# A four-layer graph-attention kernel: one group's shifted scores and exponentials moved from VectorE to ScalarE, and its log-sum-exp products spread over twice as many steps

## The chip, the cores and the metric

The kernel runs on one core of a Trainium2 chip. The metric is the device time of one execution in microseconds, as the median of several runs. The engines are called as in the profile: PE (TensorE, matrix products), DVE (VectorE), ACT (ScalarE), POOL (GpSimd) and SP (SyncE, which here only starts DMAs). Each engine works through its own list of instructions in order and waits on semaphores that the others raise.

## The reference, cut to what matters

There are B = 8 batches of N = 2048 nodes with F = 64 features, and one 2048 x 2048 adjacency matrix for all of them. Three graph-attention layers follow one another, then a fourth layer with a softmax per feature, and each ends in a residual sum and a layer norm. The change concerns the third attention layer (layer 2 in the code, which counts from 0):

```python
h = jnp.matmul(x, W)
f1 = jnp.einsum('bnf,f->bn', h, a1)
f2 = jnp.einsum('bnf,f->bn', h, a2)
e = jax.nn.leaky_relu(f1[:, :, None] + f2[:, None, :], negative_slope=ALPHA)
e = jnp.where(adj[None, :, :] > 0, e, NEG_BIG)
attention = jax.nn.softmax(e, axis=2)
h_prime = jnp.matmul(attention, h)
```

Its scores can be large, so the kernel needs a bound for each row before it takes exponentials. It gets one from a scaled log-sum-exp: with the largest score of a batch taken off f2 (that gives s2), it takes exp(s2 * scale + 75) for every source node, multiplies these by the 0/1 adjacency matrix on PE, and turns the sums back into a bound for each target node.

## The kernel before

**Tiles and units.** The 2048 nodes are K = 16 blocks of 128, so that a tile holds 128 nodes in its partitions. The adjacency matrix stands in SBUF as `edge`, 128 x 16 x 2048 in fp8. A unit is one layer of one batch, and it has 16 steps, one for each block jb of 128 source nodes. The order of units (`todo`) is layer 0 and layer 1 of batches 0 to 3, layer 0 and layer 1 of batches 4 to 7, and layer 2 of batches 0 to 7. "(0,6)" is layer 0 of batch 6.

**A step.** `reach` calls `weights` (lines 997 to 1005): one DVE instruction of 128 x 2048 makes the weights w of block jb as max(r, low) * edge. r is a row of scores that `spread` (line 843) has laid over all partitions in PSUM, with four small products on PE at the end of the unit before. In layer 2 ACT then takes the exponential of w. `products` (line 1044) multiplies w by the features on PE and sums into two PSUM banks, acc. At step 15 it adds the rows of empty nodes (acc<-emptyT,mean). There are four buffers for w, so DVE can be a few steps ahead of PE.

**Work beside the steps.** Everything else is written as generators, held in `bg`, a list of streams. After each step `bg.step()` (line 1513) lets each stream run to its next `yield`; `yield n` means that it is taken up again n steps later. The instructions go into the engines' lists in just this order and are kept in it (`InOrder`, line 70). So a `yield` decides between which weights instructions of DVE, and between which products of PE, a piece of side work stands. Streams are `features0` (layer 0's features), `finish` (the end of a unit: p_o, o, eh, hb, the layer norm's sq_x and st_x), `scores` (the next layer's scores: p_xT, p_s, se, p_r, then the row), `mask_out` (copies of `edge` to DRAM as float, mf) and `group`. Two PSUM buffers, handed out in order by `pm_slots`, serve all of these. `Banks.width` (line 129) says how many of them `finish` and `transposed` take at once: two, but one while `Banks.busy` is set.

**The group.** Layer 2's batches form two groups of NB = 4: batches 0 to 3 (gi = 0) and 4 to 7 (gi = 1). `group` (line 856) begins when the last `scores` of its batches are done. For the first group that is during layer 0 of batches 4 to 7, and for the second during layer 2. It does, one after the other:

- the largest and smallest f2 of each batch: lc, a transpose p_lc, lt, a product p_lim, and lim in every partition;
- eight small DVE operations on sc, among them the scale sc[:, 1] of each batch;
- s2 = f2 - lim, tt = s2 * sc[:, 1] on DVE, 128 x 64 each, and te = exp(tt + 75) on ACT, which goes into the constant tile `te` in bf16;
- six more DVE operations: down, lo, tt, lo, lo and sc[:, 3];
- a wait until unit 12, which is (1,4), and then the 256 products p_lse<-te,edge, in eight blocks of 32, with a `yield` after each;
- am: six DVE operations that turn the sums into bounds, a transpose p_am, a copy amT on ACT, five POOL operations that split it into three bf16 pieces, and a DMA to rows_d, from which `prepare` loads the row of each batch's layer 2.

While p_lse is held, one of the two PSUM buffers is taken and `Banks.busy` is set.

Of the kernel before, what the change touches and what calls it, by code (L numbers as in the profile page):

```python
# [8 lines left out]
F32 = mybir.dt.float32  # L9
# [5 lines left out]
AF = mybir.ActivationFunctionType  # L15
ALU = mybir.AluOpType
AX = mybir.AxisListType

P = 128
# [31 lines left out]
def gnn4_kernel(ctx: ExitStack, tc: tile.TileContext, t, out):  # L51
# [3 lines left out]
    K = N // P  # L55
# [3 lines left out]
    NB = 4  # L59
# [4 lines left out]
    small = ctx.enter_context(tc.tile_pool(name="small", bufs=2))  # L64
# [76 lines left out]
    pe, dve, act, pool = (InOrder(e) for e in (nc.tensor, nc.vector, nc.scalar, nc.gpsimd))  # L141

    def psum(name):
        return pm.tile([P, 512], F32, tag="pm", name=name)

    def bc_f(v, n=K, f=F):
        return v[:, :, None].to_broadcast([P, n, f])
# [75 lines left out]
    p = psum("p_nodes")  # L223
# [27 lines left out]
    te = consts.tile([P, K, NB], BF16, name="te")  # L251
# [105 lines left out]
    lse_up = consts.tile([P, 1], F32, name="lse_up")  # L357
# [498 lines left out]
    def group(gi):  # L856

        bs = list(range(gi * NB, (gi + 1) * NB))
        g = groups2[gi]
        nm = f"g{gi}"  # L860
        s = g.s
# [6 lines left out]
        p = psum(f"p_lc_{nm}")  # L868
# [7 lines left out]
        p = psum(f"p_lim_{nm}")  # L876
# [7 lines left out]
        yield 1  # L884
        lim = small.tile([P, 2, NB], F32, tag="lim", name=f"lim_{nm}")
        dve.tensor_copy(lim, p[:, : 2 * NB].rearrange("p (a b) -> p a b", a=2))
        pm_slots.give()

        sc = small.tile([P, 4, NB], F32, tag="sc", name=f"sc_{nm}")
# [11 lines left out]
        )  # L901
        yield 1
        g.s2 = small.tile([P, NB, K], F32, tag="s2", name=f"s2_{nm}")
        dve.tensor_tensor(g.s2, s[:, 1], bc_f(lim[:, 0], NB, K), ALU.subtract)
        tt = small.tile([P, NB, K], F32, tag="tt", name=f"tt_{nm}", bufs=1)
        dve.tensor_tensor(tt, g.s2, bc_f(sc[:, 1], NB, K), ALU.mult)
        act.activation(
            te.rearrange("p k b -> p b k"), tt, AF.Exp, bias=lse_up
        )

        g.down = small.tile([P, NB, K], F32, tag="down", name=f"down_{nm}")
        dve.tensor_scalar(g.down, g.s2, -SHIFT, None, ALU.add)
# [16 lines left out]
        p = psum(f"p_lse_{nm}")  # L929
        for ib in range(K):  # L930
            for jb in range(K):
                pe.matmul(
                    p[:, NB * ib : NB * (ib + 1)],
                    lhsT=edge[:, jb, ib * P : (ib + 1) * P],
                    rhs=te[:, jb, :],
                    start=(jb == 0),
                    stop=(jb == K - 1),
                )
            if ib % 2:
                yield 1 if gi else 2  # L940
        dve.tensor_scalar(
            am.rearrange("p b k -> p k b"),
            p[:, : NB * K].bitcast(I32).rearrange("p (k b) -> p k b", b=NB),
# [16 lines left out]
        p = psum(f"p_am_{nm}")  # L960
# [504 lines left out]
    for n, (layer, b) in enumerate(todo):  # L1465
# [10 lines left out]
        for jb in range(K):  # L1476
# [15 lines left out]
            if jb == K - 1:  # L1492
                end = [lambda u=u: finish(u)]
                if layer < 2:
                    end += [2 if now[0] < 2 else 1, lambda layer=layer, b=b: scores(layer + 1, b)]
                else:
                    end += [1, lambda b=b: l3_features(b)]
                if layer == 1 and b % NB == NB - 1:
                    end += [lambda b=b: group(b // NB)]
                bg.add(chain(*end), begun=True, slow=done)  # L1500
            elif not done and jb >= 10 and ready(*nxt):
                prepare(*nxt)
                prepared.add(n + 1)
                done = True
# [524 lines left out]
```

## Time and profile before

| what | value |
|---|---|
| runs | 1358.67 us median of 3 (1357.25 to 1359.91) |
| profiled execution, its own time | 1361.64 us |
| its span, first to last instruction | 1359.8 us |
| mean granted clock of PE | 0.959 |
| busy: PE, DVE, POOL, ACT | 1214.8, 1176.2, 813.9, 752.0 us |
| weights of layers 0 and 1 on DVE | 270 instructions, 550.9 us |
| products of layers 0 and 1 on PE | 2048 records, 495.7 us |
| first group's p_lse blocks | 567.1 to 607.9 us |
| first group's s_g and tt_g on DVE | 501.0 to 505.1 us |

In the profile a tile's name comes without its number, so `acc<-w,pv` is the product of every unit of layers 0 and 1. `s_g` is the group's s2. A line of the timeline gives the start, the duration, the engine, the operation, what it writes and reads, and in brackets the time that the engine stood idle before it and who ended that. All lines of the kernel carry one line number, L80, because every operation goes through one recording helper; one goes by the tiles' names.

### The profile page before, as it was taken

To read this page: it belongs to the slowest core of one execution; us is meant where nothing else is said; L and a number is where in the kernel's file an instruction comes from. 1 tells how busy PE (TensorE), PEld (TensorE's weight loads), DVE (VectorE), ACT (ScalarE), POOL (GpSimd) and SP (SyncE) were. 2 spreads that over 40 slices of the span, in tenths; PEclk is the share of its full clock that TensorE was granted. 3 is DMA by queue.
4 is the path that set the end of the run, shared out by engine and by line. 5 is a ranking of instruction groups with operands and counts; after the bars stand their busy time and mean duration, and the time that the engine had idled before them with its cause. 6 is when DMAs were issued, how large, how long until landed. Compare 5 with 4: busy or idle time off the path is not lost.

```text
span 1359.8 us, 19529 instructions
## 1 busy us (share of the span) xinstructions
PE 1214.8 (89%) x7169; PEld 622.8 (46%) x7169; DVE 1176.2 (87%) x1064; ACT 752.0 (55%) x1370; POOL 813.9 (60%) x1163
## 2 busy tenths in 40 slices
PE   3689897999999979999998889789998899989995
PEld 3333232344343423343333334245654555668895
DVE  3889888999999998789999889898979798978865
ACT  4444443546345553344426978777566767675432
POOL 1665876677879787657763533434464665656443
PEclk9689999999999999799999988899999999999998
DMA  8640000000000222123101000025543545534663
GB/s 292 234 106 1 1 2 1 2 2 2 2 1 1 94 64 81 59 79 96 33 1 39 1 16 1 22 63 147 142 134 94 139 117 140 139 113 140 179 167 80
DMA packets 120651, 102.98 MB, mean 76 GB/s; under 512 B 58877, under 2 KB 91805, under 8 KB 119522
## 3 DMA queue, kind: packets, MB, share of 16 engines
q1 hardware_dynamic: 120178, 101.52, 25.9%
q8 instruction: 59, 0.97, 0.3%
q14 instruction: 46, 0.38, 0.1%
q10 hardware_dynamic: 368, 0.12, 0.0%
HBM read 76.13 MB, written 25.45 MB: 75 GB/s over the span
## 4 chain that ended last, share of the span: by engine, by line
PE 49%; DVE 15%; ACT 7%; issue 7%; POOL 3%; DMA 1%; SPq 0%; DVEq 0%; POOLq 0%; ACTq 0%
PE acc L80 27%; PE p_l L80 14%; DVE w L80 8%; ACT w L80 2%; PE p_o L80 2%; PE p_s L80 2%; DVE o L80 2%; PE r L80 1%; ACT sp L80 1%; DVE x L80 1%; PE p_lse_g L80 1%; DVE nd L80 1%; DVE fs L80 1%; ACT L80 1%; PE p_h L80 1%
## 5 line engine op out<-in xcount | busy, mean ns | idle before, releaser
L80 DVE SCALAR_TENSOR_TENSOR w<-r,se,edge 128x2048 f32<-128x2048 f32 (+1 forms) x270 | 550.9, 2103 | 31.1 <-PE r L80 23.2
L80 PE MATMUL acc<-w,pv 128*64 128x512 f32 x2048 | 495.7, 618 | 41.3 <-DVE w L80 29.6
L80 DVE SCALAR_TENSOR_TENSOR w<-r,lo_g,edge 128x2048 f32<-128x2048 f32 (+1 forms) x144 | 297.3, 2097 | 28.8 <-PE r L80 16.8
L80 ACT ACTIVATE w<-w,down_g 128x2048 f32<-128x2048 f32 (+1 forms) x144 | 257.5, 1810 | 71.5 <-DVE w L80 56.9
L80 PEld LDWEIGHTS p_l<-v,mask 128*128 128x128 f32 x2048 | 252.8, 193 | 60.7 <-issue 46.2
L80 PE MATMUL acc<-w,x 128*64 128x512 f32 x1024 | 258.1, 633 | 25.2 <-ACT w L80 21.8
L80 PE MATMUL p_l<-v,mask 128*128 128x256 f32 x2048 | 268.6, 288 | 10.0 <-ACT mask L80 5.2
L80 PEld LDWEIGHTS acc<-w,pv 128*64 128x64 f32 x2048 | 133.1, 139 | 293.5 <-issue 179.9
L80 POOL TENSOR_TENSOR sq_x<-sq_x 128x32 f32<-128x32 f32 (+4 forms) x207 | 109.8, 531 | 59.1 <-ACT sq_x L80 44.5
L80 PEld LDWEIGHTS acc<-w,x 128*64 128x64 f32 x1024 | 66.2, 142 | 140.6 <-issue 86.1
L80 ACT ACTIVATE o<-p_o,den 128x64 f32<-128x64 f32 x256 | 55.8, 326 | 64.5 <-DVE den L80 64.5
L80 ACT ACTIVATE nd<-p_l,empty 128x256 f32<-128x256 f32 x64 | 29.9, 469 | 81.0 <-PE p_l L80 80.8
L80 PE MATMUL p_o<-rh,oT 128*128 128x130 f32 x384 | 60.5, 294 | 15.5 <-DVE o L80 4.9
L80 ACT COPY oT<-acc 128x512 f32<-128x512 f32 x48 | 25.7, 586 | 85.8 <-PE acc L80 85.8
L80 PEld LDWEIGHTS p_o<-rh,oT 128*128 128x128 f32 x384 | 49.5, 194 | 49.2 <-issue 26.6
L80 POOL TENSOR_TENSOR st_x<-isw_x,mhalf 128x16 f32<-128x16 f32 x24 | 70.3, 2930 | 1.9
L80 POOL TENSOR_SCALAR isw<-isw 128x4 f32<-128x4 f32 x32 | 9.0, 281 | 100.5 <-DVE isw L80 82.1
L80 POOL TENSOR_TENSOR eh<-eh,x 128x1024 f32<-128x1024 f32 (+2 forms) x24 | 36.4, 1530 | 39.5 <-ACT eh L80 35.0
L80 POOL TENSOR_TENSOR d<-x,wa_bc 128x1024 f32<-128x1024 f32 x8 | 19.1, 2382 | 66.5 <-DVE x L80 66.5
L80 DVE RECIPROCAL nd<-nd 128x256 f32<-128x256 f32 x32 | 55.8, 1743 | 0.0
L80 POOL TENSOR_TENSOR sq_x<-o 128x512 f32<-128x512 f32 x23 | 29.2, 1269 | 41.4 <-DVE o L80 41.2
L80 ACT ACTIVATE xs<-x,nodes 128x64 f32<-128x64 f32 x128 | 44.3, 438 | 3.5 <-PE p_xT L80 3.4
(263 smaller groups left out, 1544.4 us busy)
## 6 DMA issues: line engine op xcount, KB each, us to landing
mask<-mask_d SPq DMA_DIRECT2D x192, 256.0 KB
mask_d<-mf SPq DMA_DIRECT2D x32, 512.0 KB
raw<-in_adjT_dram SPq DMA_DIRECT2D x8, 1024.0 KB
raw<-in_adjT_dram SPq DMA_DIRECT2D x16, 512.0 KB
x<-in_x_dram SPq DMA_DIRECT2D x8, 512.0 KB
x_d<-x SPq DMA_DIRECT2D x8, 512.0 KB
e<-x_d SPq DMA_DIRECT2D x64, 64.0 KB
out_dram<-o SPq DMA_DIRECT2D x64, 64.0 KB
```

The costliest lines, as they stand in the source:

```text
L80: ins = f(*args, **kwargs)
```

## The change

For the first group alone, the two DVE operations that make s2 and tt, and the one ACT operation that makes te, are replaced by eight ACT operations of 128 x 16, four for s2 (one per batch, with the negative of the batch's largest score as bias) and four for te (with the batch's scale). The negative comes from one more DVE operation, `away`. A `yield 2` follows, so the six DVE operations after it are issued two steps later. Further down, the pause after each block of log-sum-exp products is four steps in place of two, so the eight blocks stand in units (1,4) and (1,5) and no longer in (1,4) alone; the PSUM buffer is held for as long. The second group stays as it was.

```diff
         yield 1
         lim = small.tile([P, 2, NB], F32, tag="lim", name=f"lim_{nm}")
         dve.tensor_copy(lim, p[:, : 2 * NB].rearrange("p (a b) -> p a b", a=2))
+        if not gi:
+            away = small.tile([P, NB], F32, tag="away", name=f"away_{nm}", bufs=1)
+            dve.tensor_scalar(away, p[:, :NB], -1.0, None, ALU.mult)
         pm_slots.give()
...
         g.s2 = small.tile([P, NB, K], F32, tag="s2", name=f"s2_{nm}")
-        dve.tensor_tensor(g.s2, s[:, 1], bc_f(lim[:, 0], NB, K), ALU.subtract)
         tt = small.tile([P, NB, K], F32, tag="tt", name=f"tt_{nm}", bufs=1)
-        dve.tensor_tensor(tt, g.s2, bc_f(sc[:, 1], NB, K), ALU.mult)
-        act.activation(
-            te.rearrange("p k b -> p b k"), tt, AF.Exp, bias=lse_up
-        )
+        if gi:
+            dve.tensor_tensor(g.s2, s[:, 1], bc_f(lim[:, 0], NB, K), ALU.subtract)
+            dve.tensor_tensor(tt, g.s2, bc_f(sc[:, 1], NB, K), ALU.mult)
+            act.activation(te.rearrange("p k b -> p b k"), tt, AF.Exp, bias=lse_up)
+        else:
+            for b in range(NB):
+                act.activation(g.s2[:, b], s[:, 1, b], AF.Identity, bias=away[:, b : b + 1])
+            for b in range(NB):
+                act.activation(
+                    te[:, :, b], g.s2[:, b], AF.Exp, scale=sc[:, 1, b : b + 1], bias=lse_up
+                )
+            yield 2
...
             if ib % 2:
-                yield 1 if gi else 2
+                yield 1 if gi else 4
```

## The prediction

> **What bounds the kernel now.** I read the page first: its span, the busy shares and the chain that ended last.
>
> ```profile
> span 1359.8 us, 19529 instructions
> ...
> PE 1214.8 (89%) x7169; PEld 622.8 (46%) x7169; DVE 1176.2 (87%) x1064; ACT 752.0 (55%) x1370; POOL 813.9 (60%) x1163
> ...
> PE 49%; DVE 15%; ACT 7%; issue 7%; POOL 3%; DMA 1%; SPq 0%; DVEq 0%; POOLq 0%; ACTq 0%
> ```
>
> PE and DVE are both nearly full, and ACT and POOL are not. In layers 0 and 1 a step of 128 source nodes costs PE 1.87 us (four products, start to start) and DVE 2.26 us (one weights instruction), and PE has further work between steps. So the lead changes hands inside each unit, and an edit must be priced in the unit where it stands. Next I cut the trace into units, a unit being one batch of one layer. The first group's log-sum-exp products lie in (1,4); the next row is (1,5):
>
> ```profile
> 563.52:611.02 47.50, 46.79 (x426) 19.79 (x425) 34.46 (x29) 17.09 (x41) 27.04 (x37) 0.91 0.22 68
> 611.02:651.64 40.62, 38.09 (x193) 14.86 (x192) 37.14 (x25) 17.93 (x48) 26.00 (x42) 1.00 0.26 80
> ```
>
> Columns: stretch, its length, busy us of PE, weight loads, DVE, ACT, POOL, then PE's clock. PE is full in (1,4) and idle 2.5 us in (1,5). The other place is unit (0,6), 482.00 to 522.05, where PE is busy only 32.01 of 40.05 us. There I read the timeline of DVE, of POOL and of PE:
>
> ```profile
> 498.76 2.35 DVE L80 SCALAR_TENSOR_TENSOR w<-r,se,edge 128x2048 f32<-128x2048 f32 x1
> 501.02 2.18 DVE L80 TENSOR_TENSOR s_g<-s,lim_g 128x64 f32<-128x64 f32 x1
> 503.24 1.82 DVE L80 TENSOR_TENSOR tt_g<-s_g,sc_g 128x64 f32<-128x64 f32 x1
> ```
>
> ```profile
> 500.77 2.35 POOL L80 TENSOR_TENSOR o<-o,hb 128x1024 f32<-128x1024 f32 x1
> 503.08 1.90 POOL L80 TENSOR_TENSOR pv<-y,se 128x1024 f32<-128x1024 f32 x1
> 507.55 2.36 POOL L80 TENSOR_TENSOR eh<-eh,x 128x1024 f32<-128x1024 f32 x1 [2.57 <-ACT eh L80]
> 509.88 0.45 POOL L80 TENSOR_SCALAR meanr<-mean,later 128x64 bf16<-128x64 bf16 x1
> 510.42 0.30 POOL L80 TENSOR_TENSOR mean<-mean,meanr 128x64 f32<-128x64 f32 x1
> 510.68 2.35 POOL L80 TENSOR_TENSOR o<-o,eh 128x1024 f32<-128x1024 f32 x1
> ```
>
> ```profile
> 501.16 3.34 PE L80 MATMUL acc<-w,pv 128*64 128x512 f32 x8 [3.70 <-DVE w L80]
> 504.43 0.43 PE L80 MATMUL p_mean<-tree,ones 128*128 128x64 f32 x2
> 508.66 6.41 PE L80 MATMUL acc<-w,pv 128*64 128x512 f32 x16 [3.80 <-DVE w L80]
> ```
>
> The two operations the change takes from DVE last 2.18 and 1.82 us, while the second group's tt_g, of the same shape, takes 0.226 us at 823.5. Each ends about 0.08 us after the POOL instruction beside it. PE waits 3.80 us for the weights behind them, and then runs at half speed (6.41 us for two steps, in place of 3.7).
>
> [...] The weights instruction reads r from PSUM and does not wait (2.35 us beside POOL). [...] a granted clock of 0.57 from 501.0 to 504.5, after 3.70 us idle. [...] the trace's se<-s, 128x16, takes 198 to 200 ns.
>
> **Part 1, away.** One DVE operation of 128x4 from PSUM, about 0.16 us, in front of the sc chain. One sc operation already waits 1.78 us on POOL there. If the 0.16 us pushes one more behind POOL's next instruction (1.89 us), w of step 11 starts at 500.7 and not 498.76. That decides little, because what follows is pinned by POOL (part 3). Bounds 0 and +1.9; I take 0.
>
> **Part 2, shifted scores and exponentials on ACT.** DVE loses s_g and tt_g: 2.18 + 1.82, and 0.30 waiting for te, 4.3 us in all. ACT loses te (0.44) and gains eight of 0.20, 1.6 us at most. ACT stands idle 8.66 us there, waiting for tt_g, so this is hidden; without that cover it is 1.2 us. ACT's next work, eh (two, 1.04 + 1.06), no longer waits for tt_g: it starts when o+hb ends, 503.12, and ends at 505.3. POOL's eh+x then starts at about 505.4 and not 507.55.
>
> **Part 3, the six DVE operations left behind (down, lo, tt, lo, lo, sc).** They move two steps later, after w of steps 12 and 13. Before, they ran at 504.98 to 506.35 in POOL's gap. After: w 11 to 13 end at about 505.6 (498.76 + 2.35 + 2 x 2.26), and POOL is without a gap from 505.4: eh+x to 507.74, meanr and mean to 508.7, o+eh to 511.05, hb to 513.4. [...] The first waits to 507.8. Where operations depend on each other the trace shows one getting through per POOL instruction (at 851.18 to 853.32 two DVE operations take 1.32 and 0.78 us beside two POOL ones). By that count the second lo falls behind o+eh, and w of step 14 starts at T = 511.2; at 508.7 if all six slip between the short ones; at 513.4 if the last falls behind hb too.
>
> PE meanwhile has w 12 and 13 early: acc 11 (half clock) to 504.5, p_mean to 504.9, acc 12 and 13 to 508.7, p_xT to 509.8. It then waits for w 14 (T + 2.3); w 15 is ready at T + 4.75, then r 1.0, acc 15 1.87, the mean rows 0.34, p_s 1.0, and the first product of (0,7) at T + 9.0. Before, that stood at 522.05. The gain is 522.05 - (T + 9.0) = 513.05 - T: 4.3 at T = 508.7, 1.85 at 511.2, -0.4 at 513.4. [...] acc 14 and r then take 1.3 and 0.3 us longer, so 0.6 to 1.85. I take 1.3 us.
>
> **Part 4, log-sum-exp at every fourth step.** The same 256 products, 8 blocks of 0.86 us: (1,4) loses four blocks, 3.45 us, and (1,5) gains them. What changes is idle time. Gains: PE's 1.0 us of waits for w in (1,5) fill up. At that unit's end the chain of waits shows
>
> ```profile
> 649.99 1.05 ACT oT L80 x2
> 651.16 0.22 ACT se L80
> 651.43 0.28 PE p_r L80
> ```
>
> where PE stands 1.50 us: p_r follows at once on the se it needs. In the new order half of p_s (1.4 us with its sum) stands in that place, beside the oT copies, and p_r comes one product later: -1.5. Losses: one PSUM buffer stays taken through (1,5), so p_o runs in four pieces (about 2.5 us for 2.2) and p_xT in two: +0.4. In (1,4) PE needs 1.87 + 0.86/4 = 2.09 us a step against DVE's 2.26, so over some five steps PE waits 0.8 us. Sum -1.3. The six am operations (1.4 us on DVE when POOL is still) move to the start of (1,6), where DVE stood 2.2 us for s_top, now one w later: hidden; +1.3 if POOL blocks them. Their DMAs (rows out, rows in) go behind one or two mask writes on SP; layer 2 needs its row at about 725, some 50 us later. The row of (1,7) is split later on POOL, about 10 us, with r due at 686: hidden.
>
> **Sum.** -1.3 - 1.3 = -2.6 us. Against the profiled execution's own 1361.64 (span 1359.8) that is 1359.0; the median of the runs is 3.0 lower, 1358.67, so 1356.1.
>
> **Rivals.** (a) The six slip through before o+eh (T = 508.7): -4.3 - 1.3 = -5.6, 1353.1. For: only 1.0 us of POOL's work lies between eh+x and o+eh. Against: one-for-one alternation. (b) Slower: the last of the six loses to hb, w 14 starts at 513.4, PE stands 6 us [...]: acc 14, r, acc 15 and p_s cost 1.3 + 0.8 + 0.9 + 0.5 more; 0.4 + 3.5 - 1.3 = +2.6, 1361.3. [...] For: hb follows o+eh without a gap. Against: sc does not depend on lo and may pass with it. (c) The change only re-spreads: (0,6) wins nothing and neither do the products, 1358.7.
>
> **How the numbers follow.** Forecast 0.42, (a) 0.24, (b) 0.20, (c) 0.14. About 0.2%, 2.7 us, is what a measurement of this kernel tells from no change. The forecast lies at that edge: half of it counts as faster, half as same. Faster: 0.21 + 0.24 + 0.01 = 0.46; slower: 0.10 from (b) and 0.07 from other places where POOL blocks (part 4's am) = 0.17; same 0.37. The forecast's own range is 1354.5 to 1358; with (a) and (b) and the clock's chance, 1351.5 to 1361.5.
>
> **What would show it.** In the new profile: s_g and te on ACT at 496 to 498; ACT's 8.7 us wait for tt_g gone; POOL's eh+x near 505.4; down_g about 2 us long and one lo or sc over 2 us, with w 14 near 511; PE's second 3.8 us wait later, not gone; the 1.50 us wait of p_r gone; (1,4) about 3 us shorter and (1,5) 1 longer. Wrong if DVE's six run unblocked (then faster), or if half-clock stretches, such as the 14 us from 558 (clock 0.52), come or go with the shift of a few us.

## The result, and the profile after

| | before | after |
|---|---|---|
| median of the runs, us | 1358.73 (1352.91 to 1361.45, 22 runs) | 1353.63 (1349.63 to 1360.50, 22 runs) |
| profiled execution, its own time | 1361.64 | 1350.35 |
| its span | 1359.8 | 1348.5 |
| mean granted clock of PE | 0.959 | 0.966 |

The ratio is 0.9973, with a 95% interval of 0.9963 to 0.9983: the kernel became faster, by 3.7 us as the ratio has it, or by 5.1 us at the medians. The time lies inside the wide range (1351.5 to 1361.5) but below the forecast's own (1354.5 to 1358): 2.5 us under the forecast and 0.5 us from rival (a). So much for the size; the place where the gain was expected is right, but what happened there is not what the forecast said.

The page of the kernel after: its span, the busy time of each engine, and the shares of the chain that ended last.

```profile
span 1348.5 us, 19533 instructions
...
PE 1207.3 (90%) x7169; PEld 619.3 (46%) x7169; DVE 1171.3 (87%) x1063; ACT 753.6 (56%) x1377; POOL 812.9 (60%) x1163
...
PE 48%; DVE 16%; ACT 7%; issue 6%; POOL 3%; DMA 1%; SPq 0%; POOLq 0%; DVEq 0%; ACTq 0%
```

DVE has lost 4.9 us of busy time and PE 7.5 us, with the same 7169 products on record. PE's products have become shorter, then: fewer of them ran at half clock, as the mean granted clock (0.959 before, 0.966 after) says too.

Now unit (0,6). The timeline of DVE after:

```profile
498.99 6.86 DVE L80 SCALAR_TENSOR_TENSOR w<-r,se,edge 128x2048 f32<-128x2048 f32 x3
505.77 0.19 DVE L80 TENSOR_SCALAR down_g<-s_g 128x64 f32<-128x64 f32 x1
505.86 0.19 DVE L80 TENSOR_SCALAR lo_g<-s_g 128x64 f32<-128x64 f32 x1
...
506.59 0.16 DVE L80 TENSOR_SCALAR sc_g<-sc_g 128x4 f32<-128x4 f32 x1
506.66 4.73 DVE L80 SCALAR_TENSOR_TENSOR w<-r,se,edge 128x2048 f32<-128x2048 f32 x3
```

The same stretch on POOL and on ACT:

```profile
503.32 1.91 POOL L80 TENSOR_TENSOR pv<-y,se 128x1024 f32<-128x1024 f32 x1
507.49 2.37 POOL L80 TENSOR_TENSOR eh<-eh,x 128x1024 f32<-128x1024 f32 x1 [2.26 <-ACT eh L80]
```

```profile
496.53 0.93 ACT L80 ACTIVATE s_g<-s,away_g 128x16 f32<-128x16 f32 x4
497.34 1.31 ACT L80 ACTIVATE te<-s_g,lse_up,sc_g 128x16 bf16<-128x16 f32 x4
505.27 1.06 ACT L80 ACTIVATE eh<-o 128x1024 f32<-128x1024 f32 x1 [6.62 <-POOL pv L80]
```

And on PE:

```profile
501.39 3.16 PE L80 MATMUL acc<-w,pv 128*64 128x512 f32 x8 [3.70 <-DVE w L80]
504.48 0.69 PE L80 MATMUL p_mean<-tree,ones 128*128 128x64 f32 x2
505.10 3.77 PE L80 MATMUL acc<-w,pv 128*64 128x512 f32 x16
...
515.85 1.94 PE L80 MATMUL acc<-w,pv 128*64 128x512 f32 x8
```

The six operations (down, lo, tt, lo, lo, sc) run between 505.77 and 506.75, 0.2 us each. POOL is still from 505.2 to 507.5, so nothing blocks them, and w 14 starts at 506.66. PE gets w 12 and w 13 at once: its second wait, 3.80 us before, is gone, and the two steps take 3.77 us where they took 6.41 at half clock. The first product of (0,7), the last line, starts at 515.85 and not 522.05. That is 6.2 us.

The stretches of (1,4) and (1,5) after, with the columns as before (stretch, length, busy us of the engines, PE's clock, DMA):

```profile
555.06:597.05 41.99, 39.87 (x299) 15.49 (x298) 35.96 (x24) 17.10 (x41) 27.01 (x37) 1.00 0.25 77
597.05:640.21 43.16, 41.97 (x318) 17.97 (x317) 38.33 (x30) 17.58 (x43) 24.54 (x37) 1.00 0.25 75
```

(1,4) is 5.5 us shorter and (1,5) 2.5 us longer. (1,4) had a clock of 0.91 before and has 1.00 now, so not all of this comes from the 3.45 us of products that moved.

From here on a unit is cut at the end of its last row products, `acc<-emptyT,mean`. For (0,6) before and after these are:

```profile
520.73 0.41 PE L80 MATMUL acc<-emptyT,mean 3*64 3x512 bf16 x4
```

```profile
514.52 0.41 PE L80 MATMUL acc<-emptyT,mean 3*64 3x512 bf16 x4
```

Cut so, the two profiles differ as follows (after less before, in us): up to (0,5) +0.2, (0,6) -6.4, (0,7) -1.2, (1,4) -6.6, (1,5) +3.1, (1,6) and (1,7) -0.2, layer 2 -1.0, the end after it +0.9. Together -11.2, the difference of the spans. The runs say 5. The profile of before is at the long end of its runs and that of after at the short end, and most of the -7.8 of (0,7) and (1,4) is a stretch of half clock of 13.65 us that stood there before and is absent now (the products moved out of (1,4) are the rest; e1 below, which leaves them in, and has no stretch, gives 6.1 and 1.7). The experiments had to say which of these terms belong to the change.

### The profile page after: what moved, and what is told of

It reads as the page before. It is cut to its first block, busy times and chain, and to the rows that moved or that the text cites. A ratio compares the mean times of both kernels' runs of the same rounds, so it can differ in the third digit from the quotient of the medians.

```text
span 1348.5 us, 19533 instructions
## 1 busy us (share of the span) xinstructions
PE 1207.3 (90%) x7169; PEld 619.3 (46%) x7169; DVE 1171.3 (87%) x1063; ACT 753.6 (56%) x1377; POOL 812.9 (60%) x1163
## 4 chain that ended last, share of the span: by engine, by line
PE 48%; DVE 16%; ACT 7%; issue 6%; POOL 3%; DMA 1%; SPq 0%; POOLq 0%; DVEq 0%; ACTq 0%
PE acc L80 26%; PE p_l L80 14%; DVE w L80 9%; ACT w L80 2%; PE p_o L80 2%; DVE o L80 2%; PE p_s L80 2%; PE r L80 1%; ACT sp L80 1%; DVE x L80 1%; POOL st_x L80 1%; DVE nd L80 1%; DVE fs L80 1%; PE p_lse_g L80 1%; POOL sq_x L80 1%
## 5 line engine op out<-in xcount | busy, mean ns | idle before, releaser
L80 PE MATMUL acc<-w,pv 128*64 128x512 f32 x2048 | 490.0, 611 | 38.2 <-DVE w L80 26.7
```

What stands on the lines that cost most here:

```text
L80: ins = f(*args, **kwargs)
```

## The experiments

My theory after the result: the gain is made in (0,6) alone, because the six operations fell into a gap of POOL. The gap is open because ACT's eh, which POOL's eh+x needs, waits for PE's p_mean (eh takes the buffer of tree, which p_mean reads), and p_mean stands behind step 11's products in PE's list. The rivals: the gain is a half-clock stretch that happened to be absent, or it comes from the wider spacing of the log-sum-exp products.

### Each part alone

The ScalarE part, with the pause behind it, and without the wider spacing (e1):

```diff
-                yield 1 if gi else 4
+                yield 1 if gi else 2
```

> Part 1 to 3 of the change alone: scores and exponentials on ACT with the two-step pause, log-sum-exp blocks still at every second step. Theory M (the gain is made in unit (0,6), because DVE no longer stands behind POOL there): about 4.2 us below the kernel before, near 1354.5, with the first product of (0,7) about 6 us earlier in the trace. Rival L (the gain comes from the spread products): near 1358, under 1 us below.

Measured: 1350.86 us (1347.27 to 1352.67), ratio 0.9935 (0.9920 to 0.9950).

The wider spacing alone, in the kernel before (e2):

```diff
-                yield 1 if gi else 2
+                yield 1 if gi else 4
```

> The log-sum-exp blocks at every fourth step alone, scores and exponentials as before. Theory M: 0 to 1.5 us below the kernel before, 1357.2 to 1358.7; PE's 1.50 us wait of p_r at the end of (1,5) gone. Rival L: 3.5 to 5 us below, near 1354.5.

Measured: 1359.83 us, ratio 1.0004 (0.9995 to 1.0012). The spread gives nothing by itself. To see whether it costs something beside the ScalarE part, the two kernels ran again on one chip:

> The change without the wider spacing of the log-sum-exp products, a second time, on the same chip as the whole change. If the spread costs time when it stands beside the ScalarE part: 2 to 4 us below the whole change (ratio to the kernel before about 0.994, the whole change about 0.997). If the first comparison only met more or fewer stretches of half clock: the two within 1.5 us of each other.

> The whole change again, on the same chip: ratio to the kernel before 0.997 (0.996 to 0.998 was measured). In its trace the six operations behind w 13 of unit (0,6) run in about 1.0 us and POOL's gap in front of eh+x is about 2.3 us, as in the first trace.

Measured: 1351.33 us without the spread (ratio 0.9941, 0.9925 to 0.9957) and 1353.55 us with it (0.9953, 0.9936 to 0.9971). The intervals overlap, so this pair alone does not tell the two apart. But the kernel without the spread was the shorter in both comparisons, by 2.2 and 2.8 us at the medians, and all its 12 runs on that chip lie at or below 1352.7 us, where four of the six with the spread lie above. So beside the ScalarE part the spread most likely costs time, and the ScalarE part alone would be the version to keep. In (0,6) the two profiles of the whole change repeat each other, 42.24 and 42.31 us; those of e1, with the same code there, have 43.45 and 43.50, and e2, with before's code, 48.49.

### eh set free from p_mean

In e3 the tree of batch 7 gets another buffer, so that eh need not wait for p_mean. No instruction changes its place on any engine.

```diff
-        tree = tmp.tile([P, K2, F], F32, tag="e", name=f"tree_{b}")
+        tree = tmp.tile([P, K2, F], F32, tag="xT" if b == 7 else "e", name=f"tree_{b}")
```

> The changed kernel, with the tree of batch 7 in another buffer, so that ACT's first eh of (0,5) no longer waits for PE's p_mean; every engine's order is the same. Theory M with the step that failed in the prediction (POOL's gap at 505 to 507.5 stays open only because eh waits for p_mean): eh starts near 503.5 in place of 505.3, POOL's eh+x near 505.7, one or more of DVE's six operations takes about 2 us, w of step 14 starts at 508.9 to 511.5 in place of 506.7, and the time is 2 to 4 us above the changed kernel, 1355.6 to 1357.6. Rival (eh is held by POOL's pv[...]): same trace and time as the changed kernel, near 1353.6.

Measured: 1357.51 us, ratio 0.9986 (0.9972 to 1.0000). Its timelines of ACT, of POOL and of DVE:

```profile
502.72 1.06 ACT L80 ACTIVATE eh<-o 128x1024 f32<-128x1024 f32 x1 [4.74 <-POOL o L80]
```

```profile
504.94 2.38 POOL L80 TENSOR_TENSOR eh<-eh,x 128x1024 f32<-128x1024 f32 x1 [0.40 <-ACT eh L80]
507.29 0.47 POOL L80 TENSOR_SCALAR meanr<-mean,later 128x64 bf16<-128x64 bf16 x1
507.84 0.30 POOL L80 TENSOR_TENSOR mean<-mean,meanr 128x64 f32<-128x64 f32 x1
508.10 2.35 POOL L80 TENSOR_TENSOR o<-o,eh 128x1024 f32<-128x1024 f32 x1
```

```profile
505.09 2.29 DVE L80 TENSOR_SCALAR down_g<-s_g 128x64 f32<-128x64 f32 x1
507.29 0.23 DVE L80 TENSOR_SCALAR lo_g<-s_g 128x64 f32<-128x64 f32 x1
...
508.12 2.36 DVE L80 TENSOR_SCALAR sc_g<-sc_g 128x4 f32<-128x4 f32 x1
510.39 4.72 DVE L80 SCALAR_TENSOR_TENSOR w<-r,se,edge 128x2048 f32<-128x2048 f32 x3
```

This is the forecast's picture, in the kernel in which its premise holds. eh starts when o+hb ends. POOL's gap shrinks from 2.26 to 0.40 us. down waits for eh+x, four operations slip through beside the two short ones, and sc waits for o+eh. w 14 starts at 510.39; this kernel is 0.4 us ahead of before at the start of (0,6), so T is 510.8 on before's clock, and the forecast had 511.2. The unit takes 50.13 us against 42.24 in the whole change. So the hold on eh is shown to be what keeps the gap open. What that is worth to the whole kernel is less sure: at the medians e3 is 3.9 us above the whole change, but its runs reach from 1351.62 to 1365.80, its interval overlaps that of the whole change's first comparison and just misses that of the second, and its profile has the long half-clock stretch at the end of (0,7) besides.

### No pause

The whole change without the pause behind the exponentials (e4):

```diff
-            yield 2
```

> The changed kernel without the two-step pause, so that the six DVE operations follow w of step 11. Theory M (what counts is where the six meet POOL): they start at 501.2 beside o+hb and pv, which hold them until about 505.2, w of step 12 starts at 505.5 or later, PE's second wait of 3 to 4 us comes back, and the time is near 1357. Rival (what counts is only that two operations and a wait less stand on DVE, 4.3 us): near 1353.6.

Measured: 1362.00 us, ratio 1.0007 (0.9995 to 1.0020). The timelines of DVE and of POOL:

```profile
506.00 2.15 DVE L80 TENSOR_SCALAR down_g<-s_g 128x64 f32<-128x64 f32 x1
508.08 1.94 DVE L80 TENSOR_SCALAR lo_g<-s_g 128x64 f32<-128x64 f32 x1
509.93 0.21 DVE L80 SCALAR_TENSOR_TENSOR tt_g<-s_g,sc_g 128x64 f32<-128x64 f32 x1
```

```profile
505.75 2.35 POOL L80 TENSOR_TENSOR o<-o,hb 128x1024 f32<-128x1024 f32 x1
508.06 1.90 POOL L80 TENSOR_TENSOR pv<-y,se 128x1024 f32<-128x1024 f32 x1
```

With s_g and tt_g gone, the next two operations in the list take their places beside POOL's o+hb and pv, and DVE loses 4.1 us where it lost 4.0. The unit takes 47.55 us, 48.67 in before. Taking operations off DVE gained little here, and nothing that the time of the kernel shows. What gained was that the remaining ones came two steps later, in the gap.

### Three more operations into the gap

If the gap swallows everything, the three operations on sc, one of which blocks for about 1.8 us in front of w 11, should go there too:

```diff
-        dve.tensor_scalar(sc[:, 2], sc[:, 3], ALPHA, -80.0, ALU.mult, ALU.add)
-        dve.tensor_scalar(sc[:, 2], sc[:, 2], 0.0, 40.0, ALU.max, ALU.min)
-        dve.scalar_tensor_tensor(
-            sc[:, 3], lim[:, 0], 1.0 - ALPHA, sc[:, 2], ALU.mult, ALU.add
-        )
...
             yield 2
+            late_sc()
```

`late_sc` is these three; the second group calls it at the old place. In e5 this is added to the whole change, in e7 to the ScalarE part alone.

> The whole change, with the three operations on sc that a profile shows at 1.78 to 1.98 us in front of w 11 moved behind the pause, into the open gap of POOL behind w 13. If what blocks them is POOL's full queue and the gap behind w 13 really lets everything through: they take some 0.4 us there, w 11 starts 1.8 us earlier, TensorE's wait in front of step 11 falls from 3.70 to about 1.9 us, and the end comes 1.5 to 2.5 us earlier than with the whole change. If the gap of POOL is set by p_mean, which then also comes earlier by as much, nine operations no longer fit in it: one or two of them block for 2 us behind eh+x, and the gain is 0.

> Both edits: the ScalarE part alone (spacing of the products as in the kernel before), with the three operations on sc behind the pause. If the two gains add: 1.5 to 2.5 us under the ScalarE part alone, about 1348.5 us. If the three only change places with other blocked ones: the same as the ScalarE part alone.

Measured: 1361.84 us, ratio 1.0023 (1.0012 to 1.0035), and 1360.99 us, ratio 1.0015 (1.0004 to 1.0026). Slower than before, both. DVE's timeline of the first:

```profile
505.50 1.84 DVE L80 TENSOR_SCALAR sc_g<-sc_g 128x4 f32<-128x4 f32 x2
...
507.55 2.35 DVE L80 TENSOR_SCALAR lo_g<-s_g 128x64 f32<-128x64 f32 x1
...
510.51 4.73 DVE L80 SCALAR_TENSOR_TENSOR w<-r,se,edge 128x2048 f32<-128x2048 f32 x3
```

and those of PE and POOL:

```profile
502.99 0.43 PE L80 MATMUL p_mean<-tree,ones 128*128 128x64 f32 x2
```

```profile
507.50 2.35 POOL L80 TENSOR_TENSOR eh<-eh,x 128x1024 f32<-128x1024 f32 x1 [0.40 <-ACT eh L80]
```

w 11 came earlier, and with it p_mean (502.99 to 503.4), so eh was held by nothing but o+hb, and the gap was 0.40 us. The nine operations lost 1.7 us behind pv and 2.2 us behind eh+x. Freeing DVE earlier closed the gap it was to use: the second of the two outcomes on record, but worse than the 0 I gave it. In e5 (0,6) took 45.03 us, still 3.6 less than before, so the loss against before is not in that unit; where it is, stays open. In e7, with the same code there, it took 47.77: the wait for w 14 was followed by 10.24 us of half clock, where e5 had 3.41. Both profiles had the long half-clock stretch at the end of (0,7) again, which led to the last four runs.

### The stretch at the end of (0,7)

The traces record when PE's clock was granted in full and when at half. In the 14 profiles a stretch of half clock lasts a multiple of 3.413 us (in before from 3.413 to 20.480, in after from 3.413 to 13.653), but for the last one, which the end of the program cuts off, and within a profile all begin on one grid of that spacing: in before at 500.61, 507.43 and 558.63 us, 2 and then 15 spacings apart. In these two profiles the grid lies differently: the stretch at 501.96 us in after begins 1.35 us behind a line of before's grid, each counted from the first instruction. I took the start of r, the short row products in front of step 15 of (0,7), and worked out how far behind a line of the grid it lay. In before r is this:

```profile
555.86 1.02 PE L80 MATMUL r<-row,ones 3*128 3x512 bf16 x4 [0.35 <-DVE w L80]
```

The long stretch begins at 558.63 there, so the line before it lies at 555.22, and r begins 0.64 us behind that line. For the ten profiles that existed by then:

| kernel of the profile | r behind a line, us | half clock from the next line on, us | (0,7) and (1,4) together, us |
|---|---|---|---|
| before, e3, e5, e7 | 0.64, 0.64, 0.74, 0.66 | 13.65 each | 88.97, 86.78, 87.29, 88.47 |
| e2, e4 | 0.92, 1.16 | 3.41 each | 82.80, 82.84 |
| after (twice), e1 (twice) | 3.33, 2.89, 2.74, 2.61 | none | 81.20, 81.20, 82.90, 82.90 |

To move r, a piece of the weights of (0,7) was computed a second time into the same place, which changes no value:

```diff
+        if u.layer == 0 and u.b == 7 and jb in (3, 5, 7, 9):
+            again = slice(0, 512)
+            dve.scalar_tensor_tensor(
+                w[:, again], s.r[:, again], low[:, jb : jb + 1], edge[:, jb, again],
+                ALU.max, ALU.mult,
+            )
```

(for the smaller dose: steps 5 and 9, 384 columns).

> The kernel before with useless work added: in unit (0,7), steps 3, 5, 7 and 9, a quarter of the weights (512 columns) is computed a second time into the same place, 0.6 us of VectorE each, 2.5 us in all. In the profiles so far the half-clock stretches start on a grid of 3.41 us, and a stretch of 13.65 us stood at the end of (0,7) in each of the four profiles in which r of (0,7) began 0.64 to 0.74 us behind a line of that grid (before, e3, e5, e7), 3.41 us at 0.92 and 1.16 us (e2, e4), none at 2.6 to 3.3 us (after and e1, twice each). If this position is the cause of the second loss of about 6 us: r now begins about 3.1 us behind a line, no stretch, and the kernel is 2 to 5 us faster than before in spite of the added work. If the stretch has another cause: 2.5 us slower.

> The whole change with the same 2.5 us of useless work in (0,7). By the position theory r begins 2.0 to 2.4 us behind a line (was 2.9 to 3.3), still no stretch: about 2.5 us slower than the whole change, ratio to the kernel before about 0.998 to 0.999. By the rival (any delay there has its own price): the same, so this run is the price of the added work.

> The kernel before with 1.0 us of useless work in (0,7): 384 columns of the weights a second time at steps 5 and 9. By the position theory r begins about 1.6 us behind a line, where no profile lies so far (one window at 1.16, none at 2.6): none or one window of half clock, 1 to 5 us faster than before. Otherwise 1.0 us slower.

> The whole change with 1.0 us of useless work in (0,7). By the position theory r begins 0.4 to 0.9 us behind a line, in the bad place: the stretch at the end of (0,7) appears, and the kernel is 4 to 7 us slower than the whole change, ratio to the kernel before 1.000 to 1.002. Otherwise 1.0 us slower than the whole change.

Measured:

| kernel | median, us | ratio to before | r behind a line | half clock from the next line on | (0,7) and (1,4), us |
|---|---|---|---|---|---|
| e9, before with the large dose | 1362.43 | 1.0021 (1.0011 to 1.0030) | 1.32 | 3.41 | 87.69 |
| e10, after with the large dose | 1358.29 | 1.0000 (0.9988 to 1.0012) | 2.52 | none | 84.34 |
| e11, before with the small dose | 1357.63 | 0.9992 (0.9980 to 1.0003) | 2.94 | none | 84.19 |
| e12, after with the small dose | 1358.13 | 0.9989 (0.9977 to 1.0002) | 2.18 | none | 82.50 |

The doses were larger than I had put them: (0,7) became longer by 3.1 and 1.3 us where after is compared with e10 and e12. The four new profiles agree with the position, but only e11's r (2.94) came to lie where a profile had been before; the other three (1.32, 2.18, 2.52) fell between the places known until then, and none of the four put r in the bad place, as e12 was meant to. The same 19 us of before and of e11, with the columns as before (the clock is the third number from the end):

```profile
556.00:575.00 19.00, 19.00 (x115) 8.34 (x114) 9.21 (x6) 4.85 (x14) 10.92 (x21) 0.64 0.03 8
```

```profile
556.00:575.00 19.00, 18.64 (x169) 8.46 (x166) 14.96 (x10) 5.12 (x15) 13.04 (x26) 1.00 0.17 53
```

With 1.3 us of useless work added, PE does 169 products there where it did 115 (not wholly the same ones), and the two units are 4.8 us shorter. But as a way to set the time of the kernel the position failed: e9 is 3.7 us slower where I had expected a gain, e11 is not told apart from before, e10 lies 4.7 us above the whole change for 3.1 us of work, and e12's profile had no stretch although its median is 4.5 us above that of the whole change. In e12's runs 7 lie between 1351.1 and 1355.0 us and 15 between 1357.6 and 1360.6, with none between; in the whole change 17 lie below 1354.8 and 5 above 1357.6. The profiled execution of e12, 1352.96 us, is one of its lower seven. Two levels about 6 us apart, and a share of the runs at each that the dose moved from 5 in 22 to 15 in 22. That fits a stretch that a run meets or misses by where the grid happens to lie. It is not shown which stretch it was in the runs that left no profile, and it leaves e9 unexplained.

The stretch at the end of (0,7) is also not the only one that differs between executions. Every edit stands behind the end of (0,5), and yet that end lies at 476.3 to 477.4 us in the profiles of after_again, e4, e9 and e10, and at 472.0 to 474.5 in the other ten. Those four, and no others, have 10.24 us of half clock in one piece at about 185 us. The two profiles of the whole change differ by 4.7 us in their span, and about 4.3 of them arise there. So 3 to 4 us of the profiles of e9 and e10 have nothing to do with the doses; how often that stretch occurs in their other runs is not known.

What the profiles do settle is (0,6), which neither the spread nor the doses touch. With before's code it took 48.67, 48.49, 47.85 and 47.79 us (before, e2, e9, e11), and with the change's 42.24, 42.31, 42.24 and 42.04 us (after twice, e10, e12) and 43.45 and 43.50 us (e1 twice). The gain there is 4.3 to 6.6 us in every pair. It does not come and go, but its size goes with how much of the unit falls into half clock: with before's code 10.24 to 13.65 us of it ran so, with the change's 3.41 us, and 6.83 in e1.

## Why the prediction was right and wrong

**Part 1, away.** Right. The sc chain blocked once as before (1.95 us for the two on record), and w 11 started at 498.99, 0.23 us later, as late as the unit itself.

**Part 2, the ACT part.** Hidden, as said, though the sizes were off: the four te take 1.31 us, 0.33 each, not 0.20. The claim that failed is the next one: "it starts when o+hb ends, 503.12". It started at 505.27. I had taken tt_g for the only thing that eh waited for, since it was the last to come in the profile of before. The buffer that eh writes was tree's, and p_mean, its reader, ended at about 504.9 in before, just ahead of te at 505.5. With the later condition gone, the one behind it held. In the profile after, the wait is put down to pv, which ended at the same time; the e3 run shows that it was p_mean.

**Part 3, the six operations.** The step "POOL is without a gap from 505.4" failed with it, and so T was 506.66 and not 511.2. The working behind T was good: gain = 513.05 - T gives 6.4 us at T = 506.66, and the unit became 6.4 us shorter. The one-for-one count was good too: it is from the trace, one blocked operation for each long POOL instruction (in before s_g, 2.18 us, beside o+hb, and tt_g, 1.82 us, beside pv). That any of the six could be blocked was my estimate; in e3 down was, for 2.29 us, and sc, for 2.36, and in e4 lo, for 1.94. What makes an operation wait there is not shown. In e3, T came out at 510.8, though it was sc and not the second lo that fell behind o+eh. The size in the sum, 1.3, was thus off by 5. What the forecast's T would have been worth was too high, though: in e3 10.24 us of half clock followed, in which acc 14, r and acc 15 took 4.3 us longer, where 1.6 were priced for acc 14 and r, and the unit became 1.5 us longer than in before. That price, and the dearer one of rival (b), were my estimates. In before, PE's waits of 3.70 and 3.80 us went with 3.41 and 6.83 us of half clock, from 500.61 and from 507.43; what sets that length is not shown.

**Part 4, the spread.** The sum of -1.3 was too good. The 1.50 us wait of p_r did go:

```profile
640.21 1.94 PE L80 MATMUL acc<-w,pv 128*64 128x512 f32 x8
642.08 0.28 PE L80 MATMUL p_r<-ident,se 128*16 128x128 f32 x1
642.29 1.94 PE L80 MATMUL acc<-w,pv 128*64 128x512 f32 x8
```

But over (1,4) to (1,7), in profiles without the long stretch, 163.3 us (e1, e11) stand against 162.9 (after): 0.4 us gained. Between e1 and after, (1,4) is 1.7 us shorter and (1,5) 1.4 longer, where about 3 and 1 were forecast. The stretch from the last product to the end of the program was 13.7 to 14.3 us in the six profiles without the spread (before, e1 twice, e7, e9, e11) and 14.5 to 15.8 in the eight with it. In all 14 the first 9.3 us of that, up to DVE's last operation, are the same; the difference lies behind it, where the traces show no engine at work any more. Why, I did not find. Alone the spread gave 1.0004, and beside the ScalarE part the kernel with it was the longer one. So the term of -1.3 measured zero at best.

**The sum.** -2.6 was predicted, from -1.3 and -1.3. Measured: -4.3 to -6.6 in (0,6) by the profiles, 0 or a loss for the spread, -5.1 at the medians. That the time came within 2.5 us of the forecast is in part luck: part 3 gave 5 us more than its sum, from a gap that the forecast had closed, and part 4 gave none of its 1.3. **Rival (a)**, "the six slip through", is what happened, at its price of 4.3 us and more, but for another reason than the short operations of POOL: POOL stood still. **Rival (b)** did not occur, nor **(c)**. The reservation that half-clock stretches "such as the 14 us from 558" might come or go was in place: it accounts for about 6 of the 11.2 us between the two profiles.

## What to carry to other kernels

In these traces a short DVE operation beside a long POOL instruction was often held until that ended (in before s_g for 2.18 us and tt_g for 1.82, each to 0.08 us after it), and taking those two away (e4) only handed the wait to the next in the list (down 2.15 us, lo 1.94); what paid was to put the block where POOL stood idle (about 0.2 us each). Before relying on an instruction to start earlier once its last condition is gone, list all its semaphores and buffers with their times in the old profile: the second-latest is the new start. And a difference between two single profiles is to be split by unit and cleared of half-clock stretches before any of it is put down to a change.

## What the runs showed of the hardware that was not expected

- The position of a piece of PE work with short row products against a grid of 3.413 us went with 13.65, 3.41 or no us of half clock behind it, in all 14 profiles (0.64 to 0.74, 0.92 to 1.32, and 2.18 to 3.33 us behind a line). That the position is the cause is not shown. No wait of PE in the 16 us before was above 0.35 us in before.
- A chain of causes over three engines: a buffer held by a PE product opened a 2.3 us gap on POOL, and the unit was 6.4 us shorter with six DVE operations in that gap. With eh free earlier, by e3 or by e5, the gap is 0.40 us; the unit took 50.13 and 45.03 us in place of 42.24, and the ratio to before was 0.9986 and 1.0023, against 0.9973 and 0.9953 for the whole change.
- Computing weights a second time cost more than their share of the columns. In e9 and e12 a DVE instruction of 384, 512 and 2048 columns took 0.53, 0.67 and 2.26 us from start to start, by an estimate from these 0.14 us and 1.04 ns a column. The whole one in front of a second one took 0.10 to 0.12 us more, too. Four doses of 512 columns so come to about 3.1 us, which is also what the unit grew by.
